# A graph layer's start on one node tile, and a last segment of eight groups in place of four

## The chip, the cores and the metric

The kernel runs on one core of a Trainium2 chip. The metric is device time in microseconds (us) from the first to the last instruction and the little that lies around it. A core has TensorE (PE in the profile; PEld is its weight load, which overlaps), VectorE (DVE), ScalarE (ACT), GpSimd (POOL) and SyncE (SP). SP here only starts transfers; POOL mostly starts scatters, that is, DMAs whose target rows are read from a list in SBUF. ACT also starts a few loads at the beginning.

## The reference

There are N = 12500 nodes with 128 features and 412500 edges, sorted by `dst`. With `ssp(x) = softplus(x) - log 2`:

```python
h = jnp.maximum(_layernorm(x, axis=-1), 0.0)
h = h @ W_in2f                                  # node rows
Wij = ssp(f_ij @ W_f1 + b_f1) @ W_f2 + b_f2     # 20 -> 128 -> 128, one row per edge
x_ij = h[idx_j] * (Wij * rcut_ij[:, None])      # idx_i = src, idx_j = dst
agg = segment_sum(x_ij, idx_i, num_segments=N)
out = x + ssp(agg @ W_o1 + b_o1) @ W_o2 + b_o2
```

`idx_j` is sorted, so the rows of `h` that 512 neighbouring edges need lie close together. `idx_i`, by which the sum goes, is in random order.

## The kernel before, in words

**Tiles.** Nodes lie in 98 blocks of 128 (`NBLK`); four blocks are a quad, and there are 25 quads (`NQ`). Edges lie in 806 chunks of 512 (`NCH`, `CH`); four chunks are a group, and there are 202 groups.

**Sorting by bins.** A chunk's messages are not summed at once. Each edge gets a slot in a table in HBM (`rank`, `rank_end`: one count per block of nodes, then a row number), and POOL scatters the chunk's 512 messages with four indirect DMAs (`message`, L814). The tables are per segment. `SEGS` says how many groups a segment has; its table gives each block `T` tiles of 128 rows, or `T + 1` for the blocks that the segment's own loops (an edge from a node to itself) fall into. With `SEGS = (88, 44, 30, 14, 14, 8, 4)`, lines L79 to L90 give T = 16, 9, 6, 3, 3, 2, 1, and with the extra tiles 1616, 914, 612, 310, 310, 206 and 108 tiles: 4076 in all. When a segment is full, a `Collect` reads its table back in units of up to six tiles (`load`, L852), marks for each row which node of the block it belongs to (`compare`, L865: one DVE instruction), sums by a matmul (`add`, L886, two passes for a tile, as the product is float32), and adds the quad's sum to `agg` in SBUF (`keep`, L909).

**The rows of h.** `make_h` makes a quad of `h`: statistics, normalisation, a transpose, the product with `W_in2f`, and a split into three bf16 parts, which are stored to HBM (`h3`, and one table for each quad, `h3_t`). For a chunk, `rows` loads the 32 rows of that table that start at its first `dst` (SP reads the start from `shift`), `window` marks for each edge which of the rows it takes, and `pick` multiplies the two (four matmuls, L791). `picked` moves the result out of PSUM and scales it by `rcut` (ACT, four instructions).

**A chunk's own chain.** `hidden` (PE) makes two chunks' first layer, `hidden_log` (three ACT instructions of 128x1024) and `hidden_end` (DVE, 128x1024) the softplus, `bias` puts the second layer's bias into PSUM, `value` (PE, eight matmuls) adds the second layer, `message` (DVE) multiplies it with the picked rows, and POOL scatters.

**Order.** Everything is unrolled and every engine works strictly in the order written. `step(k)` is one turn of the loop: the message of chunk k, `picked` and `value` of k+1, `pick` and `bias` of k+2, `window` of k+3, `rank` up to six chunks ahead, and the softplus two to four ahead. The loop runs from k = -3. Before it, the head makes the first steps of quad 0 (`h[0]`), the columns and ranks of chunk 0, and its softplus by hand. Quads 0 and 1 are finished inside the first steps, the other quads later (`side`), together with checks and late loads (`rest`).

**Collecting.** `at`, `end` and `rate` spread the units of segments 0 to 5 over the steps: a segment may start `DELAY` = 7 steps after its last chunk, and the last unit falls on step `NCH + BEYOND` = 820 or a little later. There are 775 such units; 36 of them, with 154 tiles, fall on steps 806 to 824, after the last message. In those steps the sums use PSUM banks of two kinds in turn (`BANKS`: "acc" and "v"), earlier only the single "acc". From step 804 `x_ahead` loads quads 14 to 24 of `x` for the output, and POOL adds the bias to them (L425).

**The end.** The last segment has 27 units. Its collection is interleaved with the output layer (`finish`), one quad behind the other: two PE passes z (L435), three ACT instructions, r (DVE, L441), eight PE passes (L445), the sum with x (DVE, L449), the store. After unit 6 every second `compare` runs on POOL as four instructions (L871).

The PSUM tag "v" has three buffers, which `bias`/`value` and `pick` share.

## Time and profile before

| | us |
|---|---|
| median of 3 runs | 5361.05 (5359.46 to 5381.23) |
| the profiled execution, time | 5381.23 |
| the profiled execution, span | 5379.5 |
| first scatter starts | 26.33 |
| last scatter starts | 5245.70 |
| first product of a collection (step 360) | 2298.4 |
| POOL's scatters, 3224 of them, busy | 3105.5 |
| POOL waits with its next scatter for DVE's message | 1257.2 |
| POOL between two scatters, nothing seen ("issue") | 855.7 |

The profiled execution is the slowest of the three, 20 us above the median. Times in what follows are from its span. An "idle before" in square brackets is how long the engine stood before that instruction, and what released it; "issue" means that nothing was seen to release it, "remote" that the releaser was not identified.

### The profile page before, as it was taken

Reading aid. Unit: us, or ns where it says so; the run is one execution under the profiler, and the core shown is the slowest. Engines: PE = TensorE matmul, PEld = TensorE weight load, DVE = VectorE, ACT = ScalarE, POOL = GpSimd, SP = SyncE. Lnnn points to the kernel's source line nnn. Section 1 sums busy time; section 2 is a strip of 40 time slices with the busy share of each in tenths; the row PEclk is TensorE's granted clock in tenths of the full one; section 3 lists DMA queues with packets and bytes.
Section 4 is the critical chain, followed back from the end, with each engine's and each line's share of the span. In section 5 each row is a group of like instructions: output and inputs, shape, how many; then the busy total and the mean of one; then the engine's idle time right before and its main releaser. Section 6 shows DMA issues by size and latency. Waiting matters only on the chain. (4 is left out here: it accounts for less than half of the span.)

```text
span 5379.5 us, 72525 instructions
## 1 busy us (share of the span) xinstructions
PE 3747.0 (70%) x21598; PEld 2865.6 (53%) x21598; DVE 3113.0 (58%) x6698; ACT 2789.4 (52%) x5464; POOL 3143.3 (58%) x3292
## 2 busy tenths in 40 slices
PE   5555565555555555588888787777777777777778
PEld 3344344433333333366666666666666556655666
DVE  5555555545444444466666666666566566666666
ACT  4555555555555555555555555455444444544443
POOL 4565666656666666666666565665555555555552
PEclk7666666666666666678888888888887788888889
DMA  4444444444433334355556555566555655565546
GB/s 137 148 149 138 145 135 139 134 124 132 111 103 97 91 111 144 116 171 178 171 179 219 158 167 169 159 190 192 165 159 160 185 174 153 169 186 158 160 135 189
DMA packets 515212, 820.54 MB, mean 153 GB/s; under 512 B 177188, under 2 KB 312728, under 8 KB 514812
## 3 DMA queue, kind: packets, MB, share of 16 engines
q1 hardware_dynamic: 411212, 602.55, 39.4%
q0 software_dynamic: 103168, 213.15, 11.8%
q8 instruction: 175, 2.87, 0.2%
q14 instruction: 225, 1.84, 0.1%
q10 hardware_dynamic: 432, 0.13, 0.0%
HBM read 419.75 MB, written 395.69 MB: 152 GB/s over the span
## 5 line engine op out<-in xcount | busy, mean ns | idle before, releaser
L814 POOL DMA_INDIRECT slots<-o,slot x3224 | 3105.5, 963 | 2137.1 <-DVE o L810 1257.2
L799 ACT ACTIVATE hg<-picked,rcut 128x128 f32<-128x128 f32 x3224 | 915.1, 366 | 1379.0 <-remote 630.8
L886 PEld LDWEIGHTS acc<-to,m 128*128 128x128 f32 x8152 | 1202.9, 229 | 485.6 <-issue 335.7
L886 PE MATMUL acc<-to,m 128*128 128x128 f32 x8152 | 1300.5, 319 | 212.8 <-issue 124.4
L783 PEld LDWEIGHTS v<-wf,r 128*128 128x128 f32 x6448 | 1092.3, 251 | 456.6 <-issue 304.8
L783 PE MATMUL v<-wf,r 128*128 128x128 f32 x6448 | 1189.1, 340 | 163.4 <-issue 85.2
L810 DVE TENSOR_TENSOR o<-v,hg 128x512 f32<-128x512 f32 x806 | 551.2, 684 | 1033.6 <-remote 451.1
L671 PE MATMUL z<-f,wf 20*128 20x512 f32 x1612 | 637.8, 872 | 505.3 <-DVE r L687 315.4
L865 DVE TENSOR_TENSOR to<-count_ps,m 128x640 f32<-128x640 f32 (+3 forms) x793 | 636.7, 826 | 256.2 <-PE acc L886 115.1
L776 ACT ACTIVATE v<-bf 128x512 f32<-128x512 f32 x804 | 484.5, 603 | 482.8 <-DVE o L810 232.6
L716 DVE TENSOR_REDUCE top<-free 128x4 f32<-128x392 f32 x806 | 448.5, 556 | 465.1 <-remote 306.9
L791 PE MATMUL picked<-near,at 96*128 96x128 bf16 x3224 | 390.3, 255 | 343.9 <-DVE o L810 260.7
L687 DVE SCALAR_TENSOR_TENSOR r<-z,nbf,a 128x1024 f32<-128x1024 f32 x403 | 514.0, 1275 | 124.1 <-ACT a L681 79.7
L744 PE MATMUL free<-inb,rest_of 128*128 128x392 f16 x806 | 330.8, 410 | 337.8 <-issue 233.7
L678 ACT ACTIVATE a<-z,bf 128x1024 f32<-128x1024 f32 x403 | 444.8, 1104 | 222.6 <-remote 98.0
L671 PEld LDWEIGHTS z<-f,wf 20*128 20x128 f32 x1612 | 158.9, 238 | 716.8 <-DVE r L687 416.7
L791 PEld LDWEIGHTS <-at 96*128 96x128 bf16 x3224 | 311.4, 117 | 399.0 <-issue 368.9
L681 ACT ACTIVATE a<-a,half 128x1024 f32<-128x1024 f32 x403 | 462.7, 1148 | 13.1
L692 DVE TENSOR_TENSOR inb<-count_ps,blk 128x392 f16<-128x392 f32 x806 | 445.3, 553 | 0.0
L679 ACT ACTIVATE a<-a 128x1024 f32<-128x1024 f32 x403 | 425.9, 1057 | 12.8
L711 PE MATMUL free<-inb,after 128*128 128x392 f16 x806 | 332.6, 413 | 8.2 <-issue 3.8
L763 DVE TENSOR_SCALAR at<-rel,prow 96x512 bf16<-96x512 bf16 x806 | 284.8, 353 | 0.0
(115 smaller groups left out, 1166.7 us busy)
## 6 DMA issues: line engine op xcount, KB each, us to landing
m<-slots SPq DMA_DIRECT2D x307, 387.0 KB
m<-slots SPq DMA_DIRECT2D x278, 322.5 KB
rel<-rel_d SPq DMA_DIRECT2D x202, 384.0 KB
slots<-o,slot POOLq DMA_INDIRECT x3224
m<-slots SPq DMA_DIRECT2D x193, 258.0 KB
slots<-zero SPq DMA_DIRECT2D x96, 387.0 KB
f<-in_f_t SPq DMA_DIRECT2D x404, 80.0 KB
slots<-zero SPq DMA_DIRECT2D x58, 516.0 KB
```

The source lines that it names most:

```text
L671: nc.tensor.matmul(z[:, k, :], wf1[rows, :], self.f[rows, :], start=True, stop=True)
L681: nc.scalar.activation(a, a, AF.Ln, bias=half, scale=0.5)
L687: nc.vector.scalar_tensor_tensor(r, z, nbf1, a, op0=ALU.max, op1=ALU.add)
L716: nc.vector.tensor_reduce(self.top[:, c * QT:(c + 1) * QT], free_v, axis=mybir.AxisListType.X, op=ALU.max)
L776: nc.scalar.activation(v, spread(bf12, QT), AF.Copy)
L783: nc.tensor.matmul(v[:, i, :], r[:, i * P:(i + 1) * P], wf2, start=False, stop=True, skip_group_check=True)
L791: nc.tensor.matmul(ps[:, i, :], at[:, i * P:(i + 1) * P], near, start=i == 0, stop=i == QT - 1, skip_group_check=True)
L799: nc.scalar.activation(hg[:, i, :], ps[:, i, :], AF.Copy, scale=self.rcut[:, j:j + 1])
L810: nc.vector.tensor_mul(o[:, :, :P], v, hg)
L814: put = nc.gpsimd.indirect_dma_start(out=views[j % VIEWS], out_offset=bass.IndirectOffsetOnAxis(ap=self.slot[:, j:j + 1], axis=0), in_=o[: ...
L865: nc.vector.tensor_tensor(to[:, :n, :], count_ps[:, None, :].to_broadcast([P, n, P]), m[:, :n, P:].to_broadcast([P, n, P]), op=ALU.is_equal)
L886: nc.tensor.matmul(self.acc[b // QT][:, i, :], m[:, j, :P], to[:, j, :], start=t == 0, stop=t == self.seg.tiles(b) - 1)
```

## The change

- **Segments.** `SEGS` becomes (88, 40, 30, 14, 14, 8, 8); `mean` counts a segment's full groups. By the same lines T is 16, 8, 6, 3, 3, 2, 2, and the tiles are 1616, 808, 612, 310, 310, 204 and 206: 4066 in all. The last segment has 49 units.
- **Collecting.** A segment may start 9 steps after its last chunk, and the units of segments 0 to 5 end with step 814: 16 units with 72 tiles are left after step 805. They use only the bank "acc"; the last segment uses both kinds in turn. `compare` and `x_bias` run on DVE alone. `x_late` gets 11 turns in the loop where it had 21; what is left of it is done after the loop.
- **The first node tile.** Block 0 goes through `make_h` alone and first (`lone`); blocks 1 to 3 follow as `h0`. Its three bf16 parts stay in SBUF (`hb_first`).
- **Six chunks pick from SBUF.** For chunks 0 to 5 (`DIRECT`), `dst` is loaded to all 128 partitions (`near_load`), `window` compares it with the partition number over 128 partitions, and `pick` uses the three parts of `hb_first`: twelve matmuls of 128 rows where there were four of 96. No rows are loaded for them. `near_check`, two reductions over 3072 numbers on one partition, runs on DVE later, in `rest`.
- **Softplus in halves.** Chunks 0 to 3 go through `hidden_half`, `logs` and DVE in halves of 128x512.
- **The head's order.** The loads, chunks 0 to 2 and the beginning of chunk 3 are written out by hand; the loop starts at k = 2. `rank` and `blocks` run two steps ahead at first and reach their old lead later. Chunks of groups 0 to 2 get their slots one chunk at a time.

```diff
-SEGS = (88, 44, 30, 14, 14, 8, 4)
+SEGS = (88, 40, 30, 14, 14, 8, 8)
...
+DIRECT = 6
+LONE = 3
...
-            mean = ((self.c1 - self.c0) * CH - (own[1] - own[0])) / QT * P / N
+            mean = (SEGS[k] * TG * P - (own[1] - own[0])) / QT * P / N
             self.T = int(ceil_div(2 * (2 * mean + 4 * (2 * mean) ** 0.5), P))
...
-            nc.sync.dma_start(xb[:, :full, :], x[q * QN:q * QN + full * P, :]
+            nc.sync.dma_start(xb[:, i0:full, :], x[q * QN + i0 * P:q * QN + full * P, :]
...
+    def near_load(a, b):
+        nc.sync.dma_start(dst_near[:, a:b, :],
+                          dst_c[a:b, :][None, :, :].to_broadcast([P, b - a, CH]))
...
+    def near_check():
+        row = dst_near[0:1, :, :].rearrange("p k e -> p (k e)")
+        over = early_row(5)[:, 1:2]
+        for i, op in enumerate((ALU.max, ALU.min)):
+            nc.vector.tensor_reduce(over, row, axis=mybir.AxisListType.X, op=op)
+            nc.vector.tensor_scalar(bad[:, NFLAG - 4 - i:NFLAG - 3 - i], over,
+                                    float(P - 1) if i == 0 else 0.0, None,
+                                    op0=ALU.is_gt if i == 0 else ALU.is_lt)
+            yield
...
-        early[0] = load_x(0)
-        part_load(0)
-        first_load(0)
-        nc.sync.dma_start(win, w_in2f)
-        for j in range(NCHUNK):
-            nc.sync.dma_start(wf1[32 * j:32 * j + RBF, :], w_f1)
+        nc.sync.dma_start(x_first[:, 0, :], x[:P, :])
+        nc.scalar.dma_start(wf1[:RBF, :], w_f1)
         nc.scalar.preload_act_table_set("natural_log_exp_and_others")
         nc.scalar.dma_start(bf1, b_f1[:, None])
         nc.scalar.dma_start(wf2, w_f2)
+        nc.scalar.dma_start(win, w_in2f)
         nc.scalar.dma_start(bf2, b_f2[None, :].to_broadcast([P, P]))
+        group(0)
+        g = groups[0]
+        g.load_f(0)
+        g.load_f(1)
+        g.load_src()
+        nc.sync.dma_start(wf1[32:32 + RBF, :], w_f1)
+        near_load(0, 1)
+        g.load_rcut()
+        near_load(1, 3)
+        for j in (2, 3):
+            g.load_f(j)
+            nc.sync.dma_start(wf1[32 * j:32 * j + RBF, :], w_f1)
+        early[0] = load_x(0)
+        first_load(0)
+        part_load(0)
+        near_load(3, DIRECT)
         make_identity(nc, ident)
         for _ in bounds(0, nc.gpsimd):
...
+        if first:
+            i0, n = 0, 1
...
             xb = load_x(q)
...
                     hb[:, lo:hi, :, :].rearrange("p c k f -> p c (k f)"))
-                if b + rows == QN:
+                if b + rows == QN and not first:
+                    kept["first"] = True
                     yield
...
-    def x_bias(xo, pieces, engine=nc.vector):
+    def x_bias(xo, pieces):
...
-            engine.tensor_add(xi, xi, spread(bo2[:p, :], xi.shape[1]))
+            nc.vector.tensor_add(xi, xi, spread(bo2[:p, :], xi.shape[1]))
...
+                self.rel = None
+                if (g + 1) * NCHUNK > DIRECT:
+                    self.rel = edge.tile([WP, NCHUNK, CH], BF16, name="rel", bufs=4)
+                    nc.sync.dma_start(self.rel, rel_d[g * NCHUNK:(g + 1) * NCHUNK, :][None, :, :]
+                                      .to_broadcast([WP, NCHUNK, CH]))
...
+                if k < DIRECT:
+                    return
...
+                    self.rcut, self.blk, self.place = (t[:, self.at] for t in (self.cols[2], blk, place))
+                    yield
...
+            def hidden_half(self, k):
+                if k % 2 == 0:
+                    self.z = psum.tile([P, 2, CH], F32, name="z")
+                rows = slice(32 * k, 32 * k + RBF)
+                nc.tensor.matmul(self.z[:, k % 2, :], wf1[rows, :], self.f[rows, :],
+                                 start=True, stop=True)
...
+            def halves(self, c):
+                z = self.z
+                a = quad.tile([P, 2, CH], F32, name="a", bufs=2)
+                r = quad.tile([P, 2, CH], F32, name="r")
+                self.pair[c] = r
+                for k in range(2):
+                    self.logs(z[:, k, :], a[:, k, :])
+                    yield
+                    nc.vector.scalar_tensor_tensor(r[:, k, :], z[:, k, :], nbf1, a[:, k, :],
+                                                   op0=ALU.max, op1=ALU.add)
+                    yield
...
+                if c == self.n - 1 or self.g < LONE:
+                    w = slice(c * QT if self.g < LONE else 0, (c + 1) * QT)
...
-                nc.vector.tensor_scalar(at, self.rel[:, c, :], prow[:WP, :], None,
-                                        op0=ALU.is_equal)
+                k = self.g * NCHUNK + c
+                at = quad.tile([P, CH], BF16, name="at")
+                if k < DIRECT:
+                    nc.vector.tensor_scalar(at, dst_near[:, k, :], node, None, op0=ALU.is_equal)
+                else:
+                    at = at[:WP, :]
...
-                if self.g * NCHUNK + c < 2:
+                if self.g * NCHUNK + c < 1:
...
-                near = self.near.pop(c)
+                if self.g * NCHUNK + c < DIRECT:
+                    parts = [hb_first[:, 0, j, :] for j in range(3)]
+                else:
+                    parts = [self.near.pop(c)]
                 for i in range(QT):
-                    nc.tensor.matmul(ps[:, i, :], at[:, i * P:(i + 1) * P], near,
-                                     start=i == 0, stop=i == QT - 1, skip_group_check=True)
+                    for j, rows in enumerate(parts):
+                        nc.tensor.matmul(ps[:, i, :], at[:, i * P:(i + 1) * P], rows,
+                                         start=i == 0 and j == 0,
+                                         stop=i == QT - 1 and j == len(parts) - 1,
+                                         skip_group_check=True)
...
+                self.banks = [("acc", 1)]
...
-                        banks = BANKS if "rest" in kept else BANKS[:1]
-                        tag, bufs = banks[b // QT % len(banks)]
+                        tag, bufs = self.banks[b // QT % len(self.banks)]
...
-        BANKS = [("acc", 1), ("v", 3)]
...
-        DELAY, BEYOND = 7, 14
...
+        def picks(k):
+            g, c = of(k)
+            ps[k] = psum.tile([P, QT, P], F32, name="picked", tag="v", bufs=3)
+            g.pick(c, ats.pop(k), ps[k])
...
-            part("rows", min(k + LW, 2 * k + 3, NEXT if k < NEXT - 3 else NCH), rows)
+            part("rows", min(k + LW, NEXT if k < NEXT - 1 else NCH) if k > 3 else DIRECT - 1, rows)
...
-            if has(k):
+            if k in vs:
...
+            if k == 3:
+                part("end", 4, pairs(hidden_end))
...
+                picks(k + 2)
                 g, c = of(k + 2)
...
-                if k + 2 > 0:
-                    bs[k + 2] = g.bias(c)
+                bs[k + 2] = g.bias(c)
...
-            part("blocks", min(k + LR + 1, 2 * k + 3), blocks)
+            part("blocks", min(k + LR + 1, k + 2 + max(0, k - 3) // 2), blocks)
...
-            upto = max(made["rank"], min(k + LR, 2 * k + 3))
+            upto = max(made["rank"], min(k + LR, k + 2 + max(0, k - 3) // 2))
...
-        at = [seg.c1 + DELAY for seg in segs[:-1]]
+        at = [seg.c1 + 9 for seg in segs[:-1]]
         work = [sum(seg.tiles(b) for b in range(NBLK)) for seg in segs[:-1]]
-        end = NCH + BEYOND
+        end = NCH + 6
...
+            yield from near_check()
...
+            lone, h0, h1 = make_h(0, psum, True), make_h(0, psum), make_h(1, psum)
+            g = groups[0]
+            next(lone)
+            next(lone)
+            biases(psum)
+            next(lone)
+            part("window", 0, window)
+            columns = g.columns()
+            next(columns)
+            next(lone)
+            g.hidden_half(0)
+            halves = g.halves(0)
+            bs[0] = g.bias(0)
+            next(lone)
+            g.blocks(0)
+            next(halves)
             ready = ranks(0)
             next(ready)
-            next(h[0])
-            part("log", 0, hidden_log)
+            next(lone)
+            picks(0)
+            hgs[0] = g.picked(0, ps.pop(0))
+            next(halves)
+            for _ in columns:
+                pass
             next(ready, None)
-            made["rank"] = 0
-            next(h[0])
-            part("rows", 1, rows)
-            biases(psum)
-            part("end", 0, hidden_end)
-            bs[0] = groups[0].bias(0)
+            vs[0] = g.value(0, bs.pop(0))
+            g.hidden_half(1)
+            g.message(0, vs.pop(0), hgs.pop(0))
+            part("window", 1, window)
+            picks(1)
+            bs[1] = g.bias(1)
+            next(halves)
+            g.blocks(1)
+            ready = ranks(1)
+            next(ready)
+            next(halves)
+            hgs[1] = g.picked(1, ps.pop(1))
+            next(ready, None)
+            vs[1] = g.value(1, bs.pop(1))
+            g.hidden_half(2)
+            part("window", 2, window)
+            picks(2)
+            g.hidden_half(3)
+            halves = g.halves(2)
+            next(halves)
+            bs[2] = g.bias(2)
+            relative(0)
+            rel_store(0)
+            early[1] = load_x(1)
             group(1)
+            group(2)
+            g.message(1, vs.pop(1), hgs.pop(1))
+            g.blocks(2)
+            ready = ranks(2)
+            next(ready)
+            next(halves)
+            hgs[2] = g.picked(2, ps.pop(2))
+            next(halves)
+            vs[2] = g.value(2, bs.pop(2))
+            next(ready, None)
+            part("window", 3, window)
+            picks(3)
+            bs[3] = g.bias(3)
+            next(halves)
+            made.update(rank=2, blocks=2, hidden=3, end=3, log=3, rows=DIRECT - 1)
+            part("hidden", 4, pairs(hidden))
+            part("window", 4, window)
+            g.message(2, vs.pop(2), hgs.pop(2))
+            for _ in range(4):
+                next(h0)
             aside = side()
-            x_early = x_ahead(early_homes(), nc.vector)
-            x_late = x_ahead(late_homes(), nc.gpsimd)
-            for k in range(-3, max(NCH, max(units) + 1)):
-                for seg, d in zeros.get(k, ()):
+            x_early, x_late = x_ahead(early_homes()), x_ahead(late_homes())
+            assert all(k > 1 for k in units)
...
+            for k in range(2, max(NCH, max(units) + 1)):
...
-                    kept["rest"] = True
                 step(k, now)
...
-                    for m in h:
-                        next(m, None)
+                if k == 3:
+                    shift(0)
+                    next(h0)
+                    next(h0)
+                for _ in range((0, 0, 0, 1, 1, 2, 2)[k] if k < 7 else 1):
+                    next(h1, None)
+                if k == 5:
+                    next(h0, None)
...
+            last.banks = [("acc", 1), ("v", 3)]
...
-                    last.compare(u + 2, nc.gpsimd if u > 6 and u % 2 else nc.vector)
+                    last.compare(u + 2)
```

In `step`, `picks` is the old `pick` of the loop under a name of its own. `columns` now stops once, after the block and place of each edge are known and before the slot starts are worked out. `load_f`, `load_src` and `load_rcut` are the old loads of a group, called one by one for group 0.

## The prediction

> **What bounds the kernel now.** I read the page first, then POOL's waits, POOL in order of time over the first 100 us, all engines over the first 30 us, and the last 140 us.
>
> ```profile
> PE 3747.0 (70%) x21598; PEld 2865.6 (53%) x21598; DVE 3113.0 (58%) x6698; ACT 2789.4 (52%) x5464; POOL 3143.3 (58%) x3292
> L814 POOL DMA_INDIRECT slots<-o,slot x3224 | 3105.5, 963 | 2137.1 <-DVE o L810 1257.2
> ...
> POOL slots L814 <- issue: 855.7, 2769, 1.3
> ```
>
> No engine is full. One scatter takes 0.96 us and the next starts 1.265 us after it, so POOL can't do a chunk in less than 4 x 1.265 = 5.06 us. The span is the first scatter's start (26.33), 3224 x 1.265 = 4078, the waits for DVE's messages and others between them (1141, the rest of 5219.4; of the 1257.2 in the page 22.3 stand ahead of the first scatter, and each of the 404 waits holds the usual 0.3), and the 133.8 from the last scatter's start to the end. The change touches the head and the tail of this; the middle keeps its steps.
>
> ```profile
> 16.26 0.39 SPq L378 DMA_DIRECT2D h<-hb  x1
> 18.89 1.52 SPq L626 DMA_DIRECT2D near<-h  x2
> 20.63 0.59 PE L791 MATMUL picked<-near,at 96*128 96x128 bf16 x4 [2.01 <-DMA near<-h]
> 23.16 2.08 PE L783 MATMUL v<-wf,r 128*128 128x128 f32 x8
> 25.34 0.69 DVE L810 TENSOR_TENSOR o<-v,hg 128x512 f32<-128x512 f32 x1 [2.67 <-PE v L783]
> 26.33 1.18 POOL L814 DMA_INDIRECT slots<-o,slot  x1 [22.34 <-DVE o L810]
> 38.29 0.96 POOL L814 DMA_INDIRECT slots<-o,slot  x1 [6.98 <-DVE o L810]
> 58.02 0.96 POOL L814 DMA_INDIRECT slots<-o,slot  x1 [4.86 <-DVE o L810]
> 82.98 0.96 POOL L814 DMA_INDIRECT slots<-o,slot  x1 [3.42 <-DVE o L810]
> ```
>
> This is the head: four tiles of h are made, stored, read back (16.26 to 20.63), then `picked`, `value`, the message. Chunk 8's first scatter is at 82.98; at POOL's pace it would be at 26.33 + 8 x 5.06 = 66.8, so 16.2 of waits lie between.
>
> ```profile
> 5272.74 1.28 DVE L865 TENSOR_TENSOR to<-count_ps,m 128x512 f32<-128x512 f32 x2
> 5273.48 2.05 PE L886 MATMUL acc<-to,m 128*128 128x128 f32 x16 [0.49 <-DVE to L865]
> 5274.67 0.69 DVE L909 TENSOR_TENSOR agg<-agg,acc 128x512 f32<-128x512 f32 x1 [0.65 <-PE acc L886]
> 5275.28 1.28 DVE L865 TENSOR_TENSOR to<-count_ps,m 128x512 f32<-128x512 f32 x2
> ...
> 5343.67 0.69 DVE L865 TENSOR_TENSOR to<-count_ps,m 128x512 f32<-128x512 f32 x1
> 5349.21 0.68 DVE L865 TENSOR_TENSOR to<-count_ps,m 128x512 f32<-128x512 f32 x1
> ...
> 5356.15 1.95 PE L886 MATMUL acc<-to,m 128*128 128x128 f32 x16
> 5359.69 1.95 PE L886 MATMUL acc<-to,m 128*128 128x128 f32 x16
> ```
>
> The tail. After the last message (5238.3) the 19 steps 806 to 824 collect a quad of two units every 2.54 us, up to 5295.6: 56.3 in all, a stall and larger units among it. Then the last segment and the output: a quad with one unit takes 5.54 / 2 = 2.77 (5343.67 to 5349.21 are two), and near the end one with two units 3.54.
>
> **The change, head.** The chain of the lone tile by rows of this head: DVE is free at 3.6 (L300 ends); statistics 0.44, ACT 0.30 + 0.20, four small DVE operations of 0.16 and one tile of L353 (0.36), with the gaps between them, end at 6.0. A quarter of the transposes (0.30), of hps (0.52) and five operations on one tile of 0.28 (as a 128x128 ACT operation takes) end at 9.0. PE goes on in its order: half of L671 (1.04), half of L772 (1.03), a rank (0.49) to 10.1, twelve picks at three times 0.59 to 11.9, eight passes of `value`, 2.08, to 14.0. Beside it ACT does half a softplus (half of 1.10 + 1.06 + 1.15) and `picked` (1.14) by 13.1, and DVE r, the slot starts and the rank by 14.0. Message 0.16 + 0.69, POOL 0.3 later: 15.3, which is **-11**. The first `near_load` lies on this path at `window` 0: some 0.8 MB is queued up to it, 3.2 us at the 252 GB/s that the stretch from 26 to 40 us moved, so it is there at about 6. It could be 2 late; the ends are -13 and -8.
>
> On the engines' queues after that: message 1 waits behind its own halves, ranks and value, 6.5 us (21.8, POOL idle 1.5), message 2 at 29.4 (2.5). Then `h0`'s four pieces stand in every queue ahead of step 2: statistics of three tiles 1.4, ACT 0.5, DVE 1.7, PE 0.9, ACT 0.5, PE 1.6, ACT 0.5, in series 7, so message 3 comes at 39.3 (POOL idle 4.9). Chunk 4's softplus is only begun in step 2 (ACT 3.3, DVE 1.27, value 2.08): idle 5. Chunk 6 is the first to need rows from HBM; the store leaves at the end of step 3 and SP's loads at step 4: idle 3. One stall of the kind that made the 3.42 at 82.98 comes on top. The sum is 20 where there were 16.2: **+4**. Ends: -16 (no wait left) and +14 (chunks 6 and 9, whose rows are loaded right behind their store, each wait the 6.98 that chunk 1 waited). What chunks 0 to 5 no longer load, SP and the DMAs did aside.
>
> `near_check`: a 1x388 reduction takes 0.545 and a 1x176 one 0.323, so 1.05 ns an element; 3072 take 3.4, twice 6.8 on DVE in two steps with `message` queued behind. DVE is busy for 55% of these steps and POOL may have four pairs of chunks in hand: 0 to +7, **+3**.
>
> The row for picks: four took 0.59 at 20.63 and 0.39 at 43.36, eight passes of `value` 2.08 and 1.06; the PEclk slices grant 0.6 to 0.7 early and 0.8 late. The Trainium skill (TensorE: Matmul & The Clock Gate, "The HAM clock gate") says that PE runs at half its clock until it was busy for about 3.4 us; the trace's 2.08 and 1.06 fit a half and a full clock. This head keeps PE busier, so by that rule picks and value of chunks 1 and 2 would take 1.2 + 1.06 in place of 1.8 + 2.08, and the head's sum would be 3 better; by the rows it is as above.
>
> **The change, middle.** Segments 0 to 5 hand 3788 tiles in 759 units to the steps before 806, where there were 3814 in 739. 26 tiles at two passes of 0.160 (the mean of L886) are 8 of PE, 20 compares of 0.68 are 14 of DVE, neither the bound by itself: -8 to +14, **0**, as from 2290 to 5239 DVE is idle for 37% and PE for 22%. Two steps less with collection change 2 x 0.3.
>
> **The change, tail.** Steps 806 to 814 remain, nine: seven quads of eight tiles and about two of twelve. With the bank "acc" alone PE can't begin before `keep` has read it: 2.05 + 0.69 + gaps, 2.83 to 3.25 as in the steps just before 5246 (agg at 5236.48, 5239.31, 5242.56). 7 x 3.05 + 2 x 4.0 and the same stall of 3.3: 33, so **-24** (-28 to -20).
>
> Eleven `x_bias` move from POOL, where they took 1.27 each beside the sums, to DVE (0.68 by L909's shape). Three fall into steps that PE sets; eight stand after the loop ahead of the first `compare` of the last segment, behind loads that SP has issued some us earlier: 5.4, **+5** (0 to +10, the upper end with one wait of 4.8 for a load, as POOL had).
>
> The last segment: 22 quads get a second unit, 2.77 to 3.54; two have twelve tiles in place of eight, one more: 22 x 0.77 + 2 x 0.95 + 0.4 = 19. But DVE, with all compares on it, needs 2 x 0.68 + 0.68 + 0.75 + 0.68 = 3.47 of each 3.54, so some rounds will be longer: 3.6, **+21** (+19 to +34, a round of 4.2).
>
> **Sum.** -11 + 4 + 3 + 0 - 24 + 5 + 21 = -2. The profiled execution took 5381.23, 1.7 more than its span, and stands 20 above the median; the terms are differences, so they go on the median: 5361 - 2 = 5359. 0.5% (27 us) is about what a measurement here tells from no change.
>
> **Rivals.**
> A. *POOL starved no longer.* Once it starts at 15.3, chunks 1 to 8 follow at 5.06 each. For it: all engines have room in the first 80 us. Against it: the serial 7 us of `h0`. The head is then -27 in place of -7: 5339, and past 27 us if the bounds of the tail help.
> B. *The head's gain is lost at the first rows from HBM.* Chunk 8 goes out at 83 as before, since rows, shift and quad 1 come as late as they did. Head 0 + 3: 5366. For it: the read-back is still there. Against it: by the sum above the store leaves near 42, and quad 1's near 65.
> C. *The last segment runs in lock step* (the slower side). DVE and PE hand each other every unit, and with two units a quad and one engine for all compares, PE's 3.54 and DVE's keep, r and sum with x (2.11) add up to 5.65: 24 x 2.88 = 69 in place of 21, 5407. It decides from a round of 4.9. For it: in the steps above PE waits 0.49 and DVE 0.65 in each 2.54. Against it: two bank kinds, and the 3.54 seen at 5356.
>
> **From these to the numbers.** The sum as it stands 0.62, A 0.14, B 0.14, C 0.10. The halves of the terms' ranges, added by squares (2.5, 15, 3.5, 11, 4, 5, 8), give 21, or 22 rounded up: 5337 to 5381, which holds A and B; C lies outside. Half of A and little of the main case are faster by over 0.5%: 0.09; C and a little: 0.11; the rest 0.80.
>
> **What would show it.** First scatter at 13 to 18; chunk 8 at 72 to 80; waits of POOL about 1 to 5 each ahead of chunks 1 to 4; no near load before 35. The last message to the last segment's first z: 45 or less where it was 62. A round of 3.5 to 3.8 in the last segment, with DVE over 90% busy. It is wrong if the early start is gone by chunk 12, if rounds take over 4.2, or if the middle's pace, 6.6 us a step, moves: a hundredth of it is 29 us.

## The result and the profile after

| | before | after |
|---|---|---|
| median, same chip (22 runs each) | 5353.89 | 5388.10 |
| ratio, 95% interval | 1 | 1.0065 (1.005 to 1.008) |
| profiled execution, time (span) | 5381.23 (5379.5) | 5405.10 (5403.4) |
| first scatter starts | 26.33 | 17.02 |
| chunk 8's first scatter | 82.98 | 90.19 |
| chunk 14's first scatter | 125.61 | 132.70 |
| chunk 360's first scatter | 2296.03 | 2296.08 |
| chunk 520's, after less before | | +22.8 |
| last message starts | 5238.3 | 5260.64 |
| last message to the end | 141.2 | 142.8 |

The kernel became slower by 0.65%, 35 us, where no change was forecast. The page after, whole engines and the two groups that matter (idle before, and what ended most of it, at the end of the line):

```profile
PE 3751.2 (69%) x21624; PEld 2882.2 (53%) x21624; DVE 3139.3 (58%) x6758; ACT 2789.7 (52%) x5476; POOL 3100.9 (57%) x3245
...
L901 POOL DMA_INDIRECT slots<-o,slot x3224 | 3097.7, 961 | 2164.6 <-DVE o L897 1280.6
...
L951 DVE TENSOR_TENSOR to<-count_ps,m 128x512 f32<-128x512 f32 (+3 forms) x824 | 646.3, 805 | 382.0 <-PE acc L966 183.2
```

DVE's and POOL's busy times moved by less than 43 us. What grew is waiting: POOL for messages from 1257.2 to 1280.6, and DVE's compares (L951, L865 before) for PE's sums from 115.1 to 183.2. Single traces must be read with care here: three executions of the same program up to chunk 359 (before, before_d8, before_r851), not all on one chip, got there after 2291, 2260 and 2239 us. So a stage is judged below by stretches in which several traces agree, and a kernel by its ratio to the kernel before on the same chip.

POOL's scatters in order of time, those with a wait of over 1 us, up to chunk 8 (in brackets the idle time before and its releaser):

```profile
17.02 1.13 POOL L901 DMA_INDIRECT slots<-o,slot  x1 [12.95 <-DVE o L897]
...
23.13 0.95 POOL L901 DMA_INDIRECT slots<-o,slot  x1 [1.21 <-DVE o L897]
...
35.25 0.96 POOL L901 DMA_INDIRECT slots<-o,slot  x1 [7.38 <-DVE st L376]
...
46.04 0.96 POOL L901 DMA_INDIRECT slots<-o,slot  x1 [5.98 <-DVE o L897]
...
56.89 0.96 POOL L901 DMA_INDIRECT slots<-o,slot  x1 [6.10 <-DVE o L897]
...
71.58 0.95 POOL L901 DMA_INDIRECT slots<-o,slot  x1 [4.68 <-DVE o L897]
...
78.97 0.96 POOL L901 DMA_INDIRECT slots<-o,slot  x1 [2.64 <-DVE o L897]
...
90.19 0.96 POOL L901 DMA_INDIRECT slots<-o,slot  x1 [6.48 <-DVE o L897]
```

The first scatter is early, as forecast. Then nearly every chunk waits: 34.5 in the lines behind the first, 35.0 with the 0.54 ahead of chunk 5, 32.6 without the usual 0.3 of each, where before had 16.2. The gain of 9.3 is a loss of 7.2 at chunk 8.

The tail on DVE, sums of a quad (L989), sums with x (L465), and compares of the last segment (L951):

```profile
5283.86 0.69 DVE L989 TENSOR_TENSOR agg<-agg,acc 128x512 f32<-128x512 f32 x1 [0.35 <-PE acc L966]
...
5286.69 0.69 DVE L989 TENSOR_TENSOR agg<-agg,acc 128x512 f32<-128x512 f32 x1 [0.68 <-PE acc L966]
...
5296.72 3.08 DVE L465 TENSOR_TENSOR xr<-xr,bo 128x512 f32<-128x512 f32 x5
5299.72 1.68 DVE L465 TENSOR_TENSOR xf<-xf,bo 128x512 f32<-128x512 f32 x4
...
5320.66 1.28 DVE L951 TENSOR_TENSOR to<-count_ps,m 128x512 f32<-128x512 f32 x2
...
5324.20 1.28 DVE L951 TENSOR_TENSOR to<-count_ps,m 128x512 f32<-128x512 f32 x2
...
5327.74 1.28 DVE L951 TENSOR_TENSOR to<-count_ps,m 128x512 f32<-128x512 f32 x2
```

A quad with the single bank takes 2.83 (5283.86 to 5286.69), the sums with x left over after the loop are nine, 4.8 us, and the last segment settles at exactly 3.54 a quad.

### The profile page after: what moved, and what is told of

Read it like the earlier page. It is cut to its first block, busy times and chain, and to the rows that moved or that the text cites. A ratio compares the mean times of both kernels' runs of the same rounds, so it can differ in the third digit from the quotient of the medians.

```text
span 5403.4 us, 72578 instructions
## 1 busy us (share of the span) xinstructions
PE 3751.2 (69%) x21624; PEld 2882.2 (53%) x21624; DVE 3139.3 (58%) x6758; ACT 2789.7 (52%) x5476; POOL 3100.9 (57%) x3245
## 5 line engine op out<-in xcount | busy, mean ns | idle before, releaser
L901 POOL DMA_INDIRECT slots<-o,slot x3224 | 3097.7, 961 | 2164.6 <-DVE o L897 1280.6
L966 PE MATMUL acc<-to,m 128*128 128x128 f32 x8132 | 1321.6, 321 | 279.0 <-issue 177.2
L864 PEld LDWEIGHTS v<-wf,r 128*128 128x128 f32 x6448 | 1104.6, 253 | 433.8 <-issue 266.2
L897 DVE TENSOR_TENSOR o<-v,hg 128x512 f32<-128x512 f32 x806 | 551.1, 684 | 889.0 <-remote 482.7
L723 PE MATMUL z<-f,wf 20*128 20x512 f32 x1604 | 617.1, 849 | 447.7 <-DVE r L750 273.3
L951 DVE TENSOR_TENSOR to<-count_ps,m 128x512 f32<-128x512 f32 (+3 forms) x824 | 646.3, 805 | 382.0 <-PE acc L966 183.2
L742 ACT ACTIVATE a<-z,bf 128x1024 f32<-128x1024 f32 (+1 forms) x405 | 445.3, 1100 | 224.3 <-remote 90.3
L876 PEld LDWEIGHTS <-at 96*128 96x128 bf16 (+1 forms) x3272 | 316.4, 118 | 428.4 <-issue 378.4
L744 ACT ACTIVATE a<-a,half 128x1024 f32<-128x1024 f32 (+1 forms) x405 | 463.3, 1144 | 13.1
L743 ACT ACTIVATE a<-a 128x1024 f32<-128x1024 f32 (+1 forms) x405 | 426.3, 1053 | 12.8
```

Source lines behind the costliest of these rows:

```text
L723: nc.tensor.matmul(z[:, k, :], wf1[rows, :], self.f[rows, :], start=True, stop=True)
L744: nc.scalar.activation(a, a, AF.Ln, bias=half, scale=0.5)
L864: nc.tensor.matmul(v[:, i, :], r[:, i * P:(i + 1) * P], wf2, start=False, stop=True, skip_group_check=True)
L876: nc.tensor.matmul(ps[:, i, :], at[:, i * P:(i + 1) * P], rows, start=i == 0 and j == 0, stop=i == QT - 1 and j == len(parts) - 1, skip_gr ...
L897: nc.vector.tensor_mul(o[:, :, :P], v, hg)
L901: put = nc.gpsimd.indirect_dma_start(out=views[j % VIEWS], out_offset=bass.IndirectOffsetOnAxis(ap=self.slot[:, j:j + 1], axis=0), in_=o[: ...
```

## Experiments

Theories at the start. **1**: the lost time lies in steps 359 to 520, in how the units of segment 0 fall on the steps. **2**: it lies in the head, and the drift between the two traces is chance. Every run has a yardstick, the kernel before on the same chip; microseconds against before are the ratio times that median.

**One half at a time.** `tail_only` is before with the diff's lines on `SEGS`, `mean`, `x_bias`, `banks`, `compare`, `at` and `end`; `head_only` is after without them.

> Before with the change's tail alone: segments 88, 40, 30, 14, 14, 8, 8, collection from nine steps behind a segment to six behind the last chunk, the bank acc alone up to the last segment, compares and sums with x on VectorE; the head is that of before. Theory 1 (the lost time lies in steps 359 to 520, in how the units of segment 0 fall on the steps): +20 to +28, of which about +20 between chunks 360 and 520 and about +4 behind the last message; the chunks up to 360 as before. Theory 2 (the head's loss stays to the end, the drift between the two traces is chance): +2 to +6, the +4 of the tail.

> Before with the change's head alone: the lone tile, the twelve picks from SBUF, the halves, the order by hand, the two reductions over the row of targets; segments, collection and tail are those of before. Theory 1: +5 to +12, all of it by chunk 13 (+7 to +12 there), nothing between chunks 360 and 520. Theory 2: +25 to +35, with chunk 13 at +7 to +12 and the rest spread over the middle. A third possibility, that DMA, ScalarE and VectorE have slack that swallows the head's loss by chunk 300 (the traces had +10 fall to -2 there): -3 to +3.

Measured: tail alone 1.0036 (1.0017 to 1.0056), +19; head alone 1.0024 (1.0001 to 1.0047), +13. Together they make 32 of the 35, the rest is within their intervals. In the head's trace chunk 14 is at +7.4 and the stretch from chunk 360 to 520 takes what it takes before (-2.3); in the tail's trace that stretch is 10.3 longer, and from the last scatter to the end it is 138.3 where before has 133.8. Neither theory holds alone: both halves lose, and what the tail loses beyond some 4 lies ahead of the last message.

**Which steps collect.** One number each.

The first two lines are `before_d8` (on before), the others `after_d8` (on after).

```diff
-        DELAY, BEYOND = 7, 14
+        DELAY, BEYOND = 8, 14
...
-        at = [seg.c1 + 9 for seg in segs[:-1]]
+        at = [seg.c1 + 8 for seg in segs[:-1]]
```

> Before with every unit of collection one step later (eight steps behind a segment in place of seven, the same rates and tiles). Between steps 359 and 440 the steps with two units are then the odd ones, which were the even ones, on which the pairs of chunks make their softplus. Theory 1 in its sharp form (it matters on which parity the double units fall): +10 to +20, gained between chunks 360 and 440 (6.47 us a chunk in place of 6.34), plus 3 for the one step more at the end. Against it (the parity does nothing, and the rate or the number of units is what counts): +2 to +4.

> After with collection eight steps behind a segment in place of nine. The units' rate is 8.54 tiles a step as before it, but in steps 359 to 400 the even steps have 1.8 units and the odd ones 1.2, where after has 1.2 and 1.7; in 440 to 480 it is 1.3 and 1.8 where after has 1.8 and 1.3. Parity: about 5 to 12 faster than after (+23 to +30 against before), chunks 360 to 440 faster and 440 to 480 slower. No parity: as after, +33 to +37.

Measured: before_d8 1.0005 (0.9983 to 1.0027), chunks 360 to 440 no slower than before (6.27 us a chunk against 6.34). The parity alone shows no cost (the interval is -9 to +14 us): the sharp form of theory 1 finds no support. after_d8 1.0039 (1.0018 to 1.0059), +21, with 6.34 in that stretch where after has 6.47. The interval overlaps that of after, so this run alone decides nothing.

**The pattern.** Each of the first 48 blocks of segment 0 has 17 tiles (the others 16) in units of 5, 6 and 6. At 8.461 tiles a step the steps alternate 5, 6+6; at 8.536 they run 5, 6+6, 5+6, 6, 5+6, 6, 5+6, 6. By the code the two part at 8.5, half of 17. One line, behind the loop that computes `rate`. `before_r851` has it on before, as shown, and the pattern slips; `tail_r846` (on tail_only) and `after_r846` (on after) have 8.461 there, and it alternates.

```diff
             end = at[j]
+        rate[0] = 8.51
```

> Before with one number set: segment 0 is collected at 8.51 tiles a step in place of 8.461. A block of it has 17 tiles in three units (5, 6, 6). Up to 8.5 tiles a step the steps alternate exactly, 5 tiles in one and 6+6 in the next; above it the pattern slips (5, 6+6, 5+6, 6, 5+6, 6 ...), as it does in after with 8.536. The work, the last step and the tail are those of before. Theory 1 in its second form (the slipping pattern of the collecting steps costs 0.1 to 0.17 us a chunk from 360 to 460): +8 to +15, seen between chunks 360 and 460. Against it (the middle's drift is chance, or comes of other things in the tail's edits): -2 to +3.

> The tail alone, but with segment 0 collected at 8.461 tiles a step as in before, so that its steps alternate 5 and 6+6 again; the segments behind it begin two steps later and the last step with collection is 816 in place of 814, about 4 us more behind the last message. Theory 1 in its second form: +6 to +12 against before (the tail alone had a median 16 above it), with chunks 360 to 460 at the pace of before. Against it: +18 to +24.

> After, with segment 0 collected at 8.461 tiles a step so that its steps alternate 5 and 6+6. Theory 1 in its second form: 8 to 13 faster than after, +20 to +28 against before, with chunks 364 to 440 at the pace of before on the same chip and not 0.1 us a chunk slower. Against it: as after, +32 to +38, and with two steps more at the end perhaps 3 above that.

Measured: before_r851 1.0020 (1.0004 to 1.0037), +11; tail_r846 1.0010 (0.9991 to 1.0029), +5, where the tail alone had +19; after_r846 1.0030 (1.0016 to 1.0043), +16, where after had +35. Three times the alternating pattern is the faster one, by 11, 14 and 19 against the yardsticks, with nearly the same work; the intervals of after and after_r846 do not meet. The 14 is no more than its own uncertainty, and after once more on a third chip (+24, below) makes 8 of the 19. So the sign is shown three times, the size is some 8 to 19. after_r846 came out below its forecast. The traces show where the wait is. VectorE's waits between the first scatters of chunks 364 and 440, those of the compares, in before and then in after (total us, times, longest):

```profile
DVE to L865 <- issue: 9.7, 15, 1.6
DVE to L865 <- PE free L711: 3.0, 2, 1.5
DVE to L865 <- PE acc L886: 0.4, 1, 0.4
```

```profile
DVE to L951 <- PE acc L966: 62.8, 19, 6.0
DVE to L951 <- remote: 36.6, 9, 6.0
...
DVE to L951 <- issue: 4.7, 8, 0.6
...
DVE to L951 <- PE free L787: 3.1, 1, 3.1
DVE to L951 <- PE v L864: 3.0, 1, 3.0
```

13 us against 110. By the same count (all releasers together) the other traces with the alternating pattern have 13 and 14 (head_only, tail_r846), 18 (after_r846), 24 (before_d8), 6 to 11 (the kernels with a mended head, below); those with the slipping pattern 81 (tail_only), 54 (before_r851) and 32 (after_d8, the one with the smaller loss). One such wait in after, DVE and PE in order of time:

```profile
2431.81 1.60 PE L966 MATMUL acc<-to,m 128*128 128x128 f32 x12
...
2433.89 0.81 DVE L951 TENSOR_TENSOR to<-count_ps,m 128x640 f32<-128x640 f32 x1
...
2434.70 0.49 PE L966 MATMUL acc<-to,m 128*128 128x128 f32 x3
...
2438.38 0.50 PE L966 MATMUL acc<-to,m 128*128 128x128 f32 x3 [0.94 <-issue]
...
2439.81 2.51 PE L966 MATMUL acc<-to,m 128*128 128x128 f32 x11 [0.92 <-issue]
...
2439.89 0.96 DVE L951 TENSOR_TENSOR to<-count_ps,m 128x768 f32<-128x768 f32 x1 [5.18 <-remote]
...
2440.83 0.68 DVE L897 TENSOR_TENSOR o<-v,hg 128x512 f32<-128x512 f32 x1
```

The step has two units. The first compare runs at 2433.89; the second stands for 5.18, while PE is at the sums of earlier units (its releaser is not named here; for 62.8 of the 110 it is PE's sum), and the message (L897) stands behind it in DVE's queue. PE is not short of time there. Twelve passes of such a sum took 1.60 at 2431.81; the next twelve are drawn out from 2434.70 to about 2440, and PE is busy for only 1.89 of the 5 us from 2435 to 2440, with nothing seen to release it ("issue"). Between chunks 364 and 440 PE stands so ahead of passes of the sums for 48 us in after and 30 in before. What makes these stretches no run tells.

**The buffers.** The compare's output `to` has three buffers. By the code, PE adds a unit one unit late, at the end of a step, so the second compare of a step needs a sum from the end of the step before, and behind a step with two units the second of two sums. Theory 3: this shortage of buffers is the cost of the pattern, and a fourth buffer takes it away.

```diff
-                to = edge.tile([P, UT, P], F32, name="to", bufs=3)
+                to = edge.tile([P, UT, P], F32, name="to", bufs=4)
```

This line on after (`after_to4`), on before (`before_to4`) and on three other kernels; `after_again` is after unchanged.

> After once more, unchanged, as the yardstick of the runs beside it: +27 to +43 against before on this chip, and between chunks 364 and 440 a pace of 6.43 us a chunk with VectorE's compares waiting 80 to 110 us there, as in the trace of after.

> After with four buffers for the one-hot tile to in place of three, nothing else. Theory 3: in the slipping pattern two steps with two units follow each other; the fourth compare then needs the buffer that PE's sum of the step before still reads, VectorE stands there (110 us of such waits between chunks 364 and 440 in after, 10 to 18 in every trace with the alternating pattern), and the slots and the message behind it are late. With the fourth buffer these waits fall below 30 and the time comes 12 to 20 below after, at +15 to +23 against before. If the compares wait for PE for another reason (PE itself late, the bank acc), the waits move to the message or stay, and the time is that of after within 5.

> Before with four buffers for the tile to. Its own compares wait 115 us for the sums and 65 without a named cause, nearly all of it behind chunk 440, where its pattern slips too. Theory 3: -5 to -20. Against it: -3 to +3.

Measured on one chip: after_again 1.0045 (1.0024 to 1.0067), +24; after_to4 0.9988 (0.9970 to 1.0006), -6; before_to4 0.9963 (0.9943 to 0.9983), -20. The compares' waits of after_to4, chunks 364 to 440:

```profile
DVE to L951 <- remote: 1.6, 1, 1.6
...
DVE to L951 <- PE v L864: 0.9, 1, 0.9
```

The waits are gone with the slipping pattern unchanged, and 30 us with them, more than forecast; before gains 20 by the same line, since its own pattern slips behind chunk 440 (its compares wait 255 us from chunk 359 to 805, 36 with four buffers; after 379, 86 with four). So the shortage of buffers is shown as the cause of the compares' waits. It is a cost of both kernels, though. Of the 24 by which after loses to before on that chip, 10 go when both have four buffers, and 14 stay (-6 against -20). Nor does the fourth buffer take away the whole cost of the pattern: PE's idle time of that kind, in the same stretch, is 10 us in before_to4 and 11 in head_best_to4 (alternating), but 28 in after_to4 and 49 and 42 in tail_to4 and mended_to4 below (slipping), and from chunk 360 to 520 the first two take 1006 and 1009 us, the others 1017, 1023 and 1032. These are single traces on two chips.

Which compares wait can be told, since the compares run in the order of the code. Of the 110 us in after, 78 stand at the second compare of a step 5+6 behind a step with one unit, 20 at that of a step 5+6 behind 6+6, and none in a step 6+6. So it is not mainly two steps with two units in a row, as the forecast of after_to4 had it. Why a step 5+6 waits where 6+6 in the alternation does not, though both stand behind a step with one unit, no run tells apart. after_again's wait in the stretch was 65 and its pace 6.38 us a chunk, below the 80 to 110 and the 6.43 expected (6.47 in the first trace of after), and its +24 is below the +27 to +43.

**The head.** Which of its waits cost? `head_rows` is head_only with quad 0 finished ahead of step 2 (six pieces in place of four), the shift behind step 2, the first rows loaded at step 3, quad 1 a step earlier. `head_both` also cuts the reductions of `near_check` into pieces of 512. `head_z` also exchanges two lines. `head_best` also puts the pieces of quad 1 and the shift behind the message and `value` of their step. `after_mended` is after_r846 with all of these.

```diff
-            part("rows", min(k + LW, NEXT if k < NEXT - 1 else NCH) if k > 3 else DIRECT - 1, rows)
+            part("rows", min(k + LW, NEXT if k < NEXT - 2 else NCH) if k > 2 else DIRECT - 1, rows)
...
-            for _ in range(4):
+            for _ in range(6):
                 next(h0)
...
-                if k == 3:
-                    shift(0)
-                    next(h0)
-                    next(h0)
-                for _ in range((0, 0, 0, 1, 1, 2, 2)[k] if k < 7 else 1):
+                if k == 2:
+                    shift(0)
+                for _ in range((0, 0, 1, 1, 2, 2)[k] if k < 6 else 1):
                     next(h1, None)
```

The two lines exchanged in `head_z`:

```diff
-            g.hidden_half(3)
             halves = g.halves(2)
             next(halves)
+            g.hidden_half(3)
```

And in `head_best`, within `step`, in place of the lines behind it:

```diff
                 vs[k + 1] = g.value(c, bs.pop(k + 1))
+            between(k)
...
+            def between(k):
+                if k == 3:
+                    shift(0)
+                for _ in range((0, 0, 0, 1, 1, 2, 2)[k] if k < 7 else 1):
+                    next(h1, None)
```

> The head alone, but the last two pieces of the quad 0 are made ahead of step 2, the shift behind step 2, the first rows are loaded at step 3 in place of 4, and the pieces of quad 1 stand one step earlier, with the rows behind chunk 8 loaded from step 6 on. If the waits for rows are what the head loses (PE waited 8.49 for chunk 6's rows and 7.03 for chunk 9's in after): POOL's waits of 4.7 ahead of chunk 6 and 6.5 ahead of chunk 8 go down to 1 or 2 each, chunk 14 at about 0 against before in place of +7, and the median 6 to 10 below that of the head alone (+3 to +7). If the head loses to the engines' queues and not to the rows, the waits move to the chunks beside: chunk 14 stays at +5 to +8, the median as the head alone, +10 to +15.

> As the run with the earlier rows, and the two reductions over 3072 targets are cut into pieces of 512, one in a step, so that no message stands behind 3.33 us of VectorE. The two reductions as they were stand ahead of waits of 6.86 and 1.72 of POOL at chunks 12 and 13: if they are the cause of these, chunk 14 comes 3 to 7 earlier than with the earlier rows alone and the median is -4 to +3 against before; if POOL's queue covers them, no difference to the run with the earlier rows.

> The run with the earlier rows and the reductions in pieces, and one pair of lines exchanged: the softplus of chunk 2 is put ahead of the first layer of chunk 3. In the traces ScalarE's first instruction on chunk 2's half waits for the end of chunk 3's matmuls (27.45), not of its own (24.05), and POOL waits 7.4 ahead of chunk 2. If that wait is what I missed there: POOL's wait ahead of chunk 2 is 3.5 to 4.5, chunk 2 goes out at 31.5 to 32.5, all later chunks 3 earlier, the median 2 to 4 below the run without the exchange, -4 to -8 against before. If VectorE and PE are what chunk 2 waits for, the time of its first scatter stays within 1 of 35.2.

> As the run with the exchange, and the pieces of quad 1 and the shift stand behind the message and the value of their step in place of ahead of the next message (message 3 stood behind 2.8 us of them on VectorE, message 6 behind 2.7). If the head's waits come of what stands ahead of the messages in VectorE's queue: POOL's waits ahead of chunks 3 and 6 shrink by 2 to 3 each, chunk 14 at -8 to -4 against before, the median -6 to -14. If PE or ScalarE sets these steps, the waits move by a chunk and the sum stays.

> After with all of these: the head as in the run before this one and segment 0 at 8.461. The head's and the middle's losses would then be gone and the tail's +4 to +8 left: -6 to +6 against before. If the tail's edits cost something else in the middle that the pattern does not explain, +8 to +16.

| | ratio (95%) | us | chunk 14 against before |
|---|---|---|---|
| head_only | 1.0024 (1.0001 to 1.0047) | +13 | +7.4 |
| head_rows | 1.0005 (0.9985 to 1.0024) | +3 | +2.4 |
| head_both | 0.9985 (0.9966 to 1.0005) | -8 | -0.9 |
| head_z | 1.0005 (0.9989 to 1.0021) | +3 | -2.2 |
| head_best | 1.0001 (0.9983 to 1.0018) | +1 | -6.8 |
| after_mended | 1.0003 (0.9989 to 1.0018) | +2 | -7.9 |

By the traces the mendings bring chunk 14 forward by 5.0, 3.3, 1.3 and 4.6, in turn. Such steps are near what chance does: the seven traces with the head of before reach chunk 14 between 122.3 and 125.6, the six with that of after between 129.5 and 133.0. The loss of some 7 is clear of that, a step of 1 or 3 by itself is not. With the earlier rows the waits also moved: POOL's wait ahead of chunk 8 fell from 8.1 to 3.5, but those ahead of chunks 3 and 6 grew from 5.7 to 9.2 and from 4.8 to 6.9, where 1 or 2 had been expected at chunk 6. The medians follow for the whole: after_r846 at +16 becomes after_mended at +2 on one chip. They can't tell single steps of 3 us apart, and neither head_z's -4 to -8 nor head_best's -6 to -14 came; head_both, forecast at -4 to +3, came out at -8. With the pattern and the head both mended, nearly all of after's loss is gone. Three views of after's head show the mended places. Chunk 6's rows, the first from HBM:

```profile
54.39 0.40 SPq L417 DMA_DIRECT2D h<-hb  x1
...
55.41 2.31 SPq L660 DMA_DIRECT2D f<-in_f_t  x4
...
57.76 0.33 SPq L652 DMA_DIRECT2D rel<-rel_d  x1
...
59.23 3.33 SPq L675 DMA_DIRECT2D near<-h  x3
...
63.08 0.61 PE L876 MATMUL picked<-near,at 96*128 96x128 bf16 x4 [8.49 <-DMA near<-h]
```

The store left at 54.39, the loads for the next group stood ahead of the rows on SP, and PE waited 8.49 for them, to 63.08. The reductions on DVE:

```profile
116.42 3.33 DVE L212 TENSOR_REDUCE early_room<-early_room 1x1 f32<-1x3072 int32 x1
...
120.24 0.68 DVE L897 TENSOR_TENSOR o<-v,hg 128x512 f32<-128x512 f32 x1
...
123.24 3.33 DVE L212 TENSOR_REDUCE early_room<-early_room 1x1 f32<-1x3072 int32 x1
...
126.68 0.69 DVE L897 TENSOR_TENSOR o<-v,hg 128x512 f32<-128x512 f32 x1
```

Each stands 3.33 us ahead of a message. Cut into pieces (head_both against head_rows), POOL's waits ahead of chunks 12 and 13 go from 6.74 and 1.70 to 3.59 and under 1. And chunk 2's softplus:

```profile
21.98 2.07 PE L732 MATMUL z<-f,wf 20*128 20x512 f32 x2
...
25.38 2.07 PE L732 MATMUL z<-f,wf 20*128 20x512 f32 x2
...
27.48 0.69 ACT L742 ACTIVATE a<-z,bf 128x512 f32<-128x512 f32 x1 [7.32 <-PE z L732]
```

Its own first layer ends at 24.05, yet ACT starts at 27.48, with the end of chunk 3's: the log was written behind both halves of the tile z. With the two lines exchanged it started at 24.04. What was left of POOL's waits up to chunk 8 with all mendings (head_best), those over 2 us; two more are 1.42 and 1.51:

```profile
30.88 0.96 POOL L905 DMA_INDIRECT slots<-o,slot  x1 [4.57 <-DVE st L380]
...
42.06 0.96 POOL L905 DMA_INDIRECT slots<-o,slot  x1 [6.36 <-DVE o L901]
...
49.95 0.96 POOL L905 DMA_INDIRECT slots<-o,slot  x1 [3.13 <-DVE o L901]
...
66.64 0.96 POOL L905 DMA_INDIRECT slots<-o,slot  x1 [5.76 <-DVE o L901]
...
81.32 0.96 POOL L905 DMA_INDIRECT slots<-o,slot  x1 [3.65 <-DVE o L901]
```

They are shorter, not gone: POOL still stands for the messages, so most of these chunks still take longer than the 5.06 us that POOL needs.

**Together.** The mended head on before's segments with four buffers, the tail alone with four buffers, and after mended with four buffers and its own rate.

> The mended head on the segments and tail of before, with four buffers for the tile to: what the other run with four buffers gives, and 0 to 7 more from the head (chunk 14 at -7 against before): -8 to -25 by theory 3, -8 to +2 against it.

> The change's tail alone on the head of before, with four buffers for the tile to. If the shortage of these buffers is all that the tail's edits lose ahead of the last message, what is left against before with four buffers (-19.6) is the +4 behind the last scatter: -20 to -12 against before. If the new segments or the later start of collection cost something of their own, -8 to +2.

> After with the mended head and four buffers for the tile to, segment 0 at its 8.536 tiles a step. After with four buffers was at -6; the head's mending was worth 14 (after with the alternating pattern +16, with the mended head too +2). So -24 to -14. Near 0 would say that the two gains are one and the same.

Measured: head_best_to4 0.9952 (0.9927 to 0.9978), -25, the fastest of all: it beats both kernels on its chip, though before_to4 (-20) can't be told from it. tail_to4 0.9999 (0.9982 to 1.0015), -1; mended_to4 0.9993 (0.9976 to 1.0011), -4. These two ran on another chip, and both miss their forecasts by more than 10. In their traces the compares' waits are as small as in the other runs with four buffers (81 and 92 from chunk 359 to 805), so either the tail's edits cost something else (PE's idle time above, 49 and 42 us, would fit), or the waits are worth less on a chip whose kernel before takes 5362 and not 5301. No run here has before_to4 on that chip, so this stays open. If before gained 20 there too, the tail would lose with four buffers what it lost with three.

## Why the prediction was wrong

Forecast -2, measured +35. By its own terms:

| term | forecast | measured |
|---|---|---|
| first scatter | -11 (-13 to -8) | -9.3 |
| POOL's waits up to chunk 8 | +4 (-16 to +14) | +16.5 |
| `near_check` | +3 | about +3.3 (chunk 14, head_both against head_rows; traces of one head differ by as much) |
| middle | 0 (-8 to +14) | +15 (tail alone +19, less some 4 behind the last scatter) |
| last message to the last segment's first z | -24 + 5 = -19 | 61.8 to 48.1: -13.7 |
| last segment and output | +21 (+19 to +34) | 79.4 to 94.7: +15.3 |

**The step that failed first is "The change, middle": 0.** It priced 26 tiles and 20 compares by their busy time and let idle shares of 37% and 22% hide them. The count was right and beside the point. What changed is in which steps the units fall: rate 8.536 lies just above 8.5, where the units no longer alternate and second compares of a step come upon three buffers that are all in use. Setting the rate alone back gave 14 of the tail's 19, and 8 to 19 in after; the compares' waits in the stretch looked at went from 81 and 110 to 14 and 18. What the tail's edits cost beyond that stays open. An engine with a third of its time free still loses when an instruction at the head of its queue waits for a buffer and the message stands behind it. The prediction said that it would be wrong if the middle's pace moved; it had not worked out the sequence of units, which the code gives.

**Second, POOL's waits in the head**, 16.5 where +4 was forecast and +14 was the upper end. Chunk by chunk: message 2 waited 7.4 and not 2.5 (the log behind both halves of z: with the lines exchanged it was 4.7); chunk 3 6.0 and chunk 4 6.1, where 5 each had been forecast; chunk 6 4.7 and not 3, as the queue on SP held back its rows; 2.6 at chunk 7, which was not foreseen; and at chunk 8 6.5 in place of one stall of 3.4. The serial picture was right, the sizes too small. Rival B named a part of it, rows read back from HBM, and set chunk 8 at 83; it came at 90. But chunk 5's first scatter was already at 62.2 against 64.7, so 6.8 of the 9.3 were gone ahead of any chunk with rows from HBM. Rival A, POOL starved no longer, did not occur. That head_only loses 13 (1 to 25) agrees with +7 at chunk 14 within its interval.

**What held.** The early start, though by its own test (gone by chunk 12) it was lost by chunk 6. `near_check`, as far as 3 us can be told. The tail as a sum, but by luck: +2 forecast, +1.6 measured, its two terms each 5 to 6 too large with opposite signs. (The 56.3 in its working is 57.3 by its own ends, 5238.3 and 5295.6; the -24 fits the latter.) The single bank gave 2.83 as well as 3.73 and 4.57 a quad, so the 3.05 was too little; nine sums with x remained and not eight, in 4.8 where 5 had been set. The last segment runs at 3.54 a quad and not in lock step (rival C): from 5319 to 5372 PE is busy all the time and DVE 89%.

**The rule on the clock.** Eight passes of `value` took 2.07 and 2.05 for chunks 1 and 2, and twelve picks 1.46 to 1.49: the rows of before decide, and the 3 us that the rule would have given are not there. The Trainium skill (TensorE: Matmul & The Clock Gate, "The HAM clock gate") would have had PE at full speed after some 3.4 us of sustained work; PE was busy for 21.4 of the 25 us from 10 to 35, for 8.23 without a break from 19.98 to 28.21, and the passes stayed long.

## What to carry to other kernels

When work is spread over the steps of an unrolled pipeline by a rate, write out the sequence that the rate gives and count the buffers that each of its steps needs; a rate just past the one at which the units alternate can cost more than the work it moves, and one more buffer may be worth as much as the placement, for the kernel before too. An early start is worth only what the next chunks can keep: look at the longest chain of each following chunk, and at which instruction a tile's reader is put behind. Idle share hides work of an engine only if nothing that waits stands ahead of the critical instruction in its queue.

## What was not expected of the hardware

Chips differ by more than the change: the kernel before had medians of 5301, 5301, 5347, 5362 and 5365 on the five chips of the experiments, so kernels were compared on one chip only. Executions of one kernel on one chip spread by 7 to 16 us (standard deviation). Traces that share the program up to chunk 359 are up to 52 us apart there, though not all on one chip; in the middle POOL either goes on at 5.06 us a chunk or loses mostly 2 to 5 at once.

The granted clock fits PE's passes in the head where the trace has records of it. In after it is 0.50 from 46.6 to 53.3, 1.00 from 53.4 to 56.7 and 0.50 from 57 to 70; eight passes of `value` took 2.08 at 49.86, 1.05 at 53.53 and 2.08 at 66.28. The first record begins at 43.2 us. For 10 to 35 us the view shows 1.00 only because nothing is recorded there, and the passes of 2.07 and 2.05 are the better witness.
